# Four half-size pairs at the end of a routed expert layer, and a new place for the weight load

## The chip, the cores and the metric

The kernel runs on one core of one Trainium2 chip. The metric is the device time of one execution in microseconds (us), the median over several runs.

## The reference, cut to what matters

The input is 64 graphs of 256 nodes with 256 features. Two layers follow each other; each is a graph attention step and a feed-forward step, both with a layer norm ahead and a residual added behind. The feed-forward step of the second layer is a mixture of 8 experts, and each token goes to its two best ones:

```python
logits = tokens @ router_w.T
probs = softmax(logits)
rw, re = top_k(probs, 2);  rw = rw / rw.sum(-1, keepdims=True)
combine = zeros((N, E)).at[arange(N)[:, None], re].set(rw)
out = tokens
for e in range(E):                                  # E = 8, D = 256
    h = gelu(tokens @ w1[e] + b1[e], approximate=False)
    y = h @ w2[e] + b2[e]
    out = out + combine[:, e:e + 1] * y
```

The reference computes all experts for all tokens. The kernel computes only the two that count, except for the last three graphs.

## The kernel before, in words

**Graphs.** `batch_layers` takes one graph (256 rows, `NT` = 2 tiles of 128) through the first layer, the second attention and the router's logits. The base of the result (`base`, the token itself) is stored to `out` from there. The first 61 graphs (`ROUTED`) are routed. The last three (`DENSE`) are computed by `dense_expert` with every expert, weighted and summed in SBUF into `dbase`, and stored by `store_dense` at L1075 when the eighth expert is done.

**Routing.** The 61 routed graphs come in chunks of 4, 2 or 1. For each chunk `route` finds the two experts of each token and its place in the expert's region of the DRAM buffer `xs`; `send` (L1094, on POOL) writes the rows there, one indirect DMA of 128 rows at a time. A row of `xs` holds 256 features, the token's number, an expert and two weights.

**Pairs.** Work on experts is cut into pairs: two tiles of 128 rows of one expert (`PAIR` = 256 rows). After a chunk, `allot` computes on DVE which pairs are full, and gives their experts and places as `ids` and `ef`; SP loads them into registers at L919 and L923. As 61 graphs have 61·256 tokens with two rows each, there are 122 pairs' worth of rows. `jobs` hands out full pairs as soon as they are certain to exist, which comes to 122 − 7 = 115. What remains lies in partly filled pairs; after the last chunk, eight writes of `fill` (L1198) put rows of weight zero behind each expert's last row, and `FLUSH` = 2·(8 − 1) = 14 more pairs are taken. Those that no expert needs read a spare region of zero-weight rows. So 129 pairs run in all, the last 14 of them the flush.

**One pair** (`expert_pair`) is, in this order: on SP four DMAs for the rows (`xr`, L930), one for the numbers and weights (`xt`, L941) and one for the expert's first weights (`we`, L959); on DVE the transposition into `sT` (L117); on PE `hidden` (four products of 128 x 256, L992); on ACT a Gelu into `hT` (L998); on PE `product` (L1007) with the resident second weights; on DVE the addition of the bias into `y` (L1017, in `result`); on ACT the scaling by the router's weight (L985); last, `scatter` on POOL.

**Adding to the result.** `scatter` (L1028) issues two indirect DMAs per pair. Each adds 128 rows of 1 KB to `out`, at the rows that `xt` names. As a token's row may occur in two pairs, both DMAs wait for the two of the pair before (`before = added[-2:] + based`): the adding of one pair starts when that of the last has landed. Nine buffers hold `y` (`YBUFS`), seven `we` (`WBUFS`), five `xr` (`XBUFS`), fourteen `xt`.

**Order.** Everything is issued in an order written by the loop at the end of the kernel (`manual_schedule`): in each step every active job goes on to its next `yield`, in the order of the ranks that they give. Each engine works through its own part of that order. Near the end (`SINGLE_AT`) one pair is begun per step while fewer than three wait for their scatter, and one dense job (an expert for one or two of the last graphs) runs beside it.

Of the kernel before, what the change touches and what calls it, by code (L numbers as in the profile page):

```python
# [9 lines left out]
F32 = mybir.dt.float32  # L10
# [5 lines left out]
P = 128  # L16
# [11 lines left out]
def kernel(  # L28
# [749 lines left out]
            dense_batch[b] = dict(base=base, xT=xT)  # L778

    XNG = 8  # L780
    dense_batch, dense_weights = {}, {}

    def dense_home(b):
# [77 lines left out]
    shift = keep.tile([P, E + 1], F32, tag="shift", name="shift")  # L861
    nc.vector.memset(shift, float(E * CAP))

    def allot(c, n, last):

        rt = lambda shape, name, bufs=2, dt=F32: chunk_tile(shape, name, c, bufs, dt)
        vec, tt = nc.vector, nc.vector.tensor_tensor
        full = rt([E], "full")  # L870
        vec.tensor_scalar(
            full, rows[0], 1.0 / PAIR, ((PAIR - 1.0 if last else 0.0) - (PAIR - 1.0) / 2) / PAIR,
            op0=ALU.mult, op1=ALU.add,
        )
        whole(full, full)
        wait = rt([E], "wait")
        tt(wait, full, used, ALU.subtract)
        yield
        ends = rt([E], "ends")
        vec.tensor_tensor_scan(ends, ones[:, :E], wait, 0.0, ALU.mult, ALU.add)  # L880
        start = rt([E], "start")
        tt(start, ends, wait, ALU.subtract)
        tt(shift[:, :E], used, start, ALU.subtract)
        took = rt([E], "took")
        vec.tensor_scalar(took, start, -1.0, float(n), op0=ALU.mult, op1=ALU.add)
        vec.scalar_tensor_tensor(took, took, 0.0, wait, op0=ALU.max, op1=ALU.min)
        tt(used, used, took, ALU.add)
        step = rt([E], "step")
        tt(step, shift[:, 1:], shift[:, :E], ALU.subtract)
        yield  # L890
        past = rt([n, E], "past")
        tt(
            past, ends[:, None, :].to_broadcast([P, n, E]),
            jrow[:, :n, None].to_broadcast([P, n, E]), ALU.is_le,
        )
        ef = rt([n], "ef", 8)
        vec.tensor_reduce(ef, past, AX.X, ALU.add)
        ids = rt([2, n], "ids", 8, I32)
        vec.tensor_scalar(ids[:, 0], ef, float(E - 1), None, op0=ALU.min)
        vec.tensor_scalar(ef, ef, float(E - 1), float(-E), op0=ALU.min, op1=ALU.add)  # L900
        yield
        tt(past, past, step[:, None, :].to_broadcast([P, n, E]), ALU.mult)
        pair_of = rt([n], "pair_of")
        vec.tensor_reduce(pair_of, past, AX.X, ALU.add)
        vec.scalar_tensor_tensor(
            pair_of, pair_of, shift[:, 0:1], jrow[:, :n], op0=ALU.add, op1=ALU.add
        )
        vec.tensor_scalar(ids[:, 1], pair_of, float(E * CAP), None, op0=ALU.min)
        yield ids, ef

    WHY = "counts of at most E (E - 1 at most), and a pair of the regions or the spare one"
    GROUP = 8

    def expert_pair(j, n, ids, ef, regs, needs):

        i = j % GROUP
        upto = min(j + GROUP, n)
        if i == 0:
            _, regs["e"] = nc.values_load_multi_w_load_instructions(  # L919
                ids[0:1, 0, j:upto], engines=[mybir.EngineType.SP], min_val=0, max_val=E - 1,  # L920
                skip_runtime_bounds_check_because=WHY,
            )
            _, regs["t"] = nc.values_load_multi_w_load_instructions(  # L923
                ids[0:1, 1, j:upto], engines=[mybir.EngineType.SP], min_val=0, max_val=E * CAP,
                skip_runtime_bounds_check_because=WHY,
            )
        e_sp, t_sp = regs["e"][i], regs["t"][i]
        xr = io.tile([P, PAIR // S, KT * S], F32, tag="xr", name="xr", bufs=XBUFS)
        loads = [
            nc.sync.dma_start(  # L930
                out=xr[g * S : (g + 1) * S],
                in_=xs_d.rearrange("(t c q) f -> t q c f", c=PAIR // S, q=S)[
                    bass.ds(t_sp, 1), :, :, g * KT * S : (g + 1) * KT * S
                ].rearrange("t q c f -> (t q) c f"),
            )
            for g in range(P // S)
        ]

        xt = small.tile([P, 2, ROW - D], F32, tag="xt", name="xt", bufs=14)
        loads.append(  # L940
            nc.sync.dma_start(  # L941
                out=xt,
                in_=xs_d.rearrange("(t k p) c -> t p k c", p=P, k=2)[
                    bass.ds(t_sp, 1), :, :, D:
                ].rearrange("t p k c -> (t p) k c"),
            )
        )
        for load in loads:
            tc.declare_no_dep(
                load.ins, query=SYNC, group="sent", keep=needs,  # L950
                reason="the pair's rows were sent by these or by sends that earlier loads waited for",
            )
            tc.add_to_no_dep_group("rows", load.ins)
            for ins in needs:
                tc.add_manual_dep(
                    load.ins, ins.name, AFTER, reason="any row of these may lie in the pair"
                )
        we = io.tile([P, WROW], F32, tag="we", name="we", bufs=WBUFS)
        nc.sync.dma_start(  # L959
            out=we, in_=wpack[bass.ds(e_sp, 1), :, :].rearrange("e p c -> (e p) c")  # L960
        )
        yield 90

        yield 95 if more else 75
        xT = turned(work.tile([P, KT, PAIR], F32, tag="sT", name="sT", bufs=3), xr)
        w = small.tile([P, 2], F32, tag="w", name="w", bufs=12)
        yield 30
        yield 30
        hT = hidden(xT, we)
        yield -65  # L970
        nc.vector.scalar_tensor_tensor(
            w[:, :, None], xt[:, :, 1:2], ef[:, j : j + 1], xt[:, :, 2:3],
            op0=ALU.is_equal, op1=ALU.mult,
        )
        nc.vector.tensor_tensor(w[:, :, None], w[:, :, None], xt[:, :, 3:4], ALU.add)
        yield 80
        if i == 0:
            _, regs["x"] = nc.values_load_multi_w_load_instructions(
                ids[0:1, 0, j:upto], engines=[mybir.EngineType.PE, mybir.EngineType.DVE],
                min_val=0, max_val=E - 1, skip_runtime_bounds_check_because=WHY,  # L980
            )
        y = result(hT, bass.ds(regs["x"][i], 1))
        yield 2
        for t in range(2):
            nc.scalar.activation(y[:, t, :], y[:, t, :], AF.Copy, scale=w[:, t : t + 1])  # L985
        scatters.append((y, xt))

    def hidden(xT, we):
        ph = bank("ph", [KT, PAIR])
        for f in range(KT):  # L990
            for k in range(KT):
                nc.tensor.matmul(  # L992
                    ph[:, f, :], we[:, k * D + f * P : k * D + (f + 1) * P], xT[:, k, :],
                    start=(k == 0), stop=(k == KT - 1),
                )
        hT = work.tile([P, KT, PAIR], F32, tag="hT", name="hT", bufs=5)
        for f in range(KT):
            nc.scalar.activation(  # L998
                hT[:, f, :], ph[:, f, :], AF.Gelu, bias=we[:, C_B1 + f : C_B1 + f + 1]
            )  # L1000
        return hT

    def product(hT, e):
        py = bank("py", [2, D])
        for t in range(2):
            for f in range(KT):
                nc.tensor.matmul(  # L1007
                    py[:, t, :], hT[:, f, t * P : (t + 1) * P],
# [4 lines left out]

    def result(hT, e):
        py = product(hT, e)
        y = io.tile([P, 2, D], F32, tag="y", name="y", bufs=YBUFS)
        nc.vector.tensor_add(y, py, b2s[:, e, :].to_broadcast([P, 2, D]))  # L1017
        return y

    scatters, added = [], []  # L1020

    def scatter():

        y, xt = scatters.pop(0)
        before = added[-2:] + based
        based.clear()
        for t in range(2):
            d = nc.gpsimd.indirect_dma_start(  # L1028
                out=out_rows, out_offset=bass.IndirectOffsetOnAxis(
                    ap=xt[:, t, 0:1].bitcast(I32), axis=0  # L1030
# [9 lines left out]
                tc.add_manual_dep(d.ins, ins.name, AFTER, reason="added to before")  # L1040
            tc.add_to_no_dep_group("out", d.ins)
            added.append(d.ins)

    GROUPS = [range(ROUTED, ROUTED + 1), range(ROUTED + 1, B)]

# [66 lines left out]
    def route(c, row0, nt, n, last, xng, lg):  # L1112
# [53 lines left out]
        second_weight(tail[:, :, 2], tail[:, :, 1])  # L1166
        for i, xe in enumerate(xng):
            vec.tensor_copy(xe[:, :, D + 1 :], tail[:, i * NT : (i + 1) * NT, :])
        parts = allot(c, n, False)
        turns = (1, 2, 4, 5) if spread else (0, 1, 2, 3) if nt == 2 * NT else (0, 0, 1, 1)  # L1170
        if last:
            ends_at = rt([E], "ends_at", 2, I32)
# [13 lines left out]
                lambda j=j: expert_pair(j, n, ids, ef, regs, needs) for j in range(n)  # L1186
            )
        if last:
            parts = allot(c + 1, FLUSH, True)
            _, ends_sp = nc.values_load_multi_w_load_instructions(  # L1190
                ends_at[0:1, :], engines=[mybir.EngineType.SP], min_val=0,
                max_val=(E * CAP - 1) * PAIR, skip_runtime_bounds_check_because="rows of a region",
# [2 lines left out]
            for e in range(E):  # L1195
# [12 lines left out]
                nc.sync.nop()  # L1208
                if e % 4 == 3:
                    yield 95  # L1210
            regs2 = {}
            waiting.extend(
                lambda j=j: expert_pair(j, FLUSH, ids2, ef2, regs2, filled)
                for j in range(FLUSH)
            )

# [19 lines left out]
                )  # L1236

    FLUSH = 2 * (E - 1)

    def jobs():  # L1240
        b = done = taken = 0
# [104 lines left out]
```

## Time and the profile before

| | |
|---|---|
| time, median of 6 runs | 1483.56 us (1476.41 to 1485.18) |
| the profiled execution, its own time | 1481.71 us |
| its span, first to last instruction | 1479.9 us (1.8 us lie around it) |
| granted TensorE clock, mean | 0.988 |
| PE busy | 1409.8 us, 95% |
| weight loads (PEld) busy | 1255.5 us, 85% |
| DVE busy | 1238.9 us, 84% |
| ACT busy | 1004.6 us, 68% |
| POOL busy | 862.1 us, 58% |
| scatters (L1028) | 258 DMAs, 414.1 us busy on POOL |

Lines such as L1028 are lines of the kernel's file. "Idle before" in a timeline is the time in which the engine stood still ahead of that instruction, with the event that the profile thinks released it. SPq and POOLq are the sequencers of those engines, which issue DMAs and wait on semaphores without counting as busy.

### The profile page before, as it was taken

The numbers are of one execution on the slowest core, as the hardware profiler recorded it, in microseconds if no ns is written. First come the engines' busy times: TensorE is split into PE (matmuls) and PEld (weight loads), VectorE is DVE, ScalarE is ACT, GpSimd is POOL, SyncE is SP. The second block draws the span as 40 slices with busy tenths as digits, with TensorE's granted clock in tenths as the row PEclk, the third lists the DMA queues.
The fourth block names the chain that finished last, engine by engine and source line by source line (L and its number), as shares of the span: only waits on it lengthen the run. The fifth ranks groups of instructions, "written<-read, shape, count | busy, mean of one in ns | idle before, by whom it ended". The sixth has DMA issues, their size and how long they took to land. (4 is left out here: it accounts for less than half of the span.)

```text
span 1479.9 us, 29895 instructions
## 1 busy us (share of the span) xinstructions
PE 1409.8 (95%) x8046; PEld 1255.5 (85%) x8046; DVE 1238.9 (84%) x4366; ACT 1004.6 (68%) x2389; POOL 862.1 (58%) x851
## 2 busy tenths in 40 slices
PE   7899999999999999999999999999999989989994
PEld 5688888889999999999999999888888878778883
DVE  7789999999999989898999999998888888765542
ACT  1477667677877787777777877677778868643331
POOL 2122446465858676766767685775666768543444
PEclk9999999999999999999999999999999999999998
DMA  4822334576778777777878776777878786798533
GB/s 129 235 86 87 104 121 118 151 186 154 189 178 202 177 186 174 186 171 179 194 185 192 175 186 145 198 186 169 203 149 191 143 181 136 152 226 167 101 44 50
DMA packets 360106, 236.20 MB, mean 160 GB/s; under 512 B 247420, under 2 KB 323204, under 8 KB 359940
## 3 DMA queue, kind: packets, MB, share of 16 engines
q1 hardware_dynamic: 307024, 158.00, 41.7%
q0 software_dynamic: 48864, 66.33, 24.0%
q10 hardware_dynamic: 4052, 9.98, 2.3%
q8 instruction: 66, 1.08, 0.3%
q14 instruction: 100, 0.82, 0.2%
HBM read 146.25 MB, written 87.94 MB: 158 GB/s over the span
## 5 line engine op out<-in xcount | busy, mean ns | idle before, releaser
L1028 POOL DMA_INDIRECT out_dram<-y,xt x258 | 414.1, 1605 | 227.8 <-issue 67.0
L595 PE MATMUL pv<-q,z 128*128 128x65 f32 (+1 forms) x2560 | 360.7, 296 | 0.4
L595 PEld LDWEIGHTS pv<-q,z 128*128 128x128 f32 x2560 | 331.4, 192 | 14.2 <-DVE z L581 0.9
L1094 POOL DMA_INDIRECT xs<-xng,pos x244 | 254.2, 1042 | 65.3 <-issue 58.3
L1007 PE MATMUL py<-w2s,hT 128*128 (+1 forms) x1224 | 283.9, 383 | 6.1 <-ACT hT L998 4.3
L1007 PEld LDWEIGHTS py<-w2s,hT 128*128 128x128 f32 x1224 | 230.4, 191 | 38.6 <-ACT hT L998 7.0
L992 PE MATMUL ph<-sT,we 128*128 128x256 f32 x1032 | 243.2, 385 | 3.3 <-DVE sT L117 1.7
L581 DVE SCALAR_TENSOR_TENSOR z<-z,q,mask 128x256 f32<-128x256 f32 x504 | 231.6, 482 | 16.0 <-DMA z<-terms 7.0
L992 PEld LDWEIGHTS ph<-sT,we 128*128 128x128 f32 x1032 | 197.0, 193 | 31.8 <-DVE sT L117 2.2
L985 ACT ACTIVATE y<-y,w 128x256 f32<-128x256 f32 x258 | 113.1, 498 | 121.1 <-DVE y L1017 120.9
L459 ACT COPY xT<-pt 128x512 f32<-128x512 f32 x209 | 121.0, 587 | 70.4 <-PE pt L453 67.9
L504 PE MATMUL pq<-wx,xT 128*128 128x259 f32 x512 | 127.1, 391 | 15.2 <-ACT xT L459 15.2
L406 POOL TENSOR_SCALAR rstd<-mv 128x4 f32<-128x4 f32 (+1 forms) x66 | 15.6, 236 | 215.8 <-DVE mv L379 165.0
L424 ACT ACTIVATE off<-x,sums 128x256 f32<-128x256 f32 x256 | 129.3, 505 | 13.2 <-DVE x L678 7.5
L1017 DVE TENSOR_TENSOR y<-py,b2s 128x512 f32<-128x512 f32 x129 | 86.0, 686 | 53.8 <-PE py L1007 42.7
L469 PE MATMUL pq<-wx,xT 128*128 128x268 f32 x512 | 128.8, 395 | 1.8 <-ACT xT L459 0.7
L504 PEld LDWEIGHTS pq<-wx,xT 128*128 128x128 f32 x512 | 96.1, 192 | 34.7 <-ACT xT L459 21.0
L998 ACT ACTIVATE hT<-ph,we 128x256 f32<-128x256 f32 x258 | 103.9, 471 | 30.8 <-PE ph L992 26.3
L671 PE MATMUL pf<-wfT,xT 128*128 128x256 f32 x512 | 122.3, 382 | 0.0
L469 PEld LDWEIGHTS pq<-wx,xT 128*128 128x128 f32 x512 | 98.4, 193 | 21.3 <-DVE wx L168 1.4
L712 ACT ACTIVATE rel<-pv,rinv 128x256 f32<-128x256 f32 x128 | 53.9, 468 | 88.2 <-DVE rinv L602 87.8
L671 PEld LDWEIGHTS pf<-wfT,xT 128*128 128x128 f32 x512 | 93.7, 193 | 10.1
(173 smaller groups left out, 2366.0 us busy)
## 6 DMA issues: line engine op xcount, KB each, us to landing
we<-wpack SPq DMA_DIRECT2D x129, 264.0 KB
xr<-xs SPq DMA_DIRECT2D x516, 64.0 KB
z<-terms SPq DMA_DIRECT2D x46, 512.0 KB
xin<-in_x_dram SPq DMA_DIRECT2D x64, 256.0 KB
out_dram<-base SPq DMA_DIRECT2D x61, 256.0 KB
xblk<-in_x_dram SPq DMA_DIRECT2D x188, 64.0 KB
z<-terms ACTq DMA_DIRECT2D x17, 512.0 KB
z<-terms SPq DMA_DIRECT2D x46, 128.0 KB
```

The lines of the kernel that those rows point to most:

```text
L424: nc.scalar.activation(off, src[:, t, :], AF.Square, bias=sums[:, t : t + 1], scale=-float(D), accum_out=sq[:, at + t : at + t + 1],)
L459: nc.scalar.copy(dst, pt)
L469: nc.tensor.matmul(pq.rearrange("p h c -> p (h c)"), xT[:, k, t * P : (t + 1) * P], wx[:, k, :], start=(k == 0), stop=(k == KT - 1),)
L504: nc.tensor.matmul(pq, xT[:, k, t * P : (t + 1) * P], wx1[:, k, :], start=(k == 0), stop=(k == KT - 1),)
L581: nc.vector.scalar_tensor_tensor(z[:, j, :, h, :], terms, q[:, j, h, HD + 2 : HD + 3], masks[0][:, j, :].rearrange("p (t i) -> p t i", t=N ...
L595: nc.tensor.matmul(pv[:, h, :], z(j, h, t), q[:, j, h, : d + 1], start=(j == 0), stop=(j == NT - 1),)
L671: nc.tensor.matmul(pf[:, t, :], xT[:, k, t * P : (t + 1) * P], wfT[:, k, :], start=(k == 0), stop=(k == KT - 1),)
L985: nc.scalar.activation(y[:, t, :], y[:, t, :], AF.Copy, scale=w[:, t : t + 1])
L992: nc.tensor.matmul(ph[:, f, :], we[:, k * D + f * P : k * D + (f + 1) * P], xT[:, k, :], start=(k == 0), stop=(k == KT - 1),)
L1007: nc.tensor.matmul(py[:, t, :], hT[:, f, t * P : (t + 1) * P], w2s[:, e, f * D : (f + 1) * D].rearrange("p e c -> p (e c)"), start=(f == 0 ...
L1028: d = nc.gpsimd.indirect_dma_start(out=out_rows, out_offset=bass.IndirectOffsetOnAxis(ap=xt[:, t, 0:1].bitcast(I32), axis=0), in_=y[:, t, ...
L1094: d = nc.gpsimd.indirect_dma_start(out=xs_d[: E * CAP * PAIR, :], out_offset=bass.IndirectOffsetOnAxis(ap=at, axis=0), in_=xe, in_offset=None,
```

## The change

It has four parts.

- The last four of the 14 flush pairs hold one tile of 128 rows in place of two. Their loads, products, Gelus, scalings and scatters cover 128 rows; each issues one scatter DMA.
- So that what is left fits, `allot_rest` takes the place of `allot` for the flush: it lists first the pairs that hold more than 128 rows (at most `WHOLE` = 10) and then those with 1 to 128.
- In `expert_pair`, for all 129 pairs, `we` is loaded ahead of `xr` and `xt`, and an `nc.sync.nop()` follows the loads.
- For the flush pairs, the load of `we` gets a dependence on the last scatter of an earlier pair, taken from a new list `ended` with one entry per scattered pair. By its name `BEHIND` it is the eleventh pair ahead.

```diff
+    BEHIND, flush_regs = 11, {}
...
+    def allot_rest(c, n):
+        rt = lambda shape, name, dt=F32: chunk_tile(shape, name + "_r", c, 1, dt)
+        vec, tt = nc.vector, nc.vector.tensor_tensor
+        base = rt([3, E], "base")
+        vec.tensor_copy(base[:, 0], used)
+        for i, more_rows in ((1, P - 1.0), (2, PAIR - 1.0)):
+            vec.tensor_scalar(
+                base[:, i], rows[0], 1.0 / PAIR, (more_rows - (PAIR - 1.0) / 2) / PAIR,
+                op0=ALU.mult, op1=ALU.add,
+            )
+        whole(base[:, 1:], base[:, 1:])
+        wait = rt([2, E], "wait")
+        tt(wait, base[:, 1:], base[:, :2], ALU.subtract)
...                                  # as in allot, over 2 * E entries in place of E
-    def expert_pair(j, n, ids, ef, regs, needs):
+    def expert_pair(j, n, ids, ef, regs, needs, tiles=2):
...
+        we = io.tile([P, WROW], F32, tag="we", name="we", bufs=WBUFS)
+        d = nc.sync.dma_start(
+            out=we, in_=wpack[bass.ds(e_sp, 1), :, :].rearrange("e p c -> (e p) c")
+        )
+        at = ROUTED * NT * P // PAIR - (E - 1) + j - BEHIND
+        if regs is flush_regs and at < len(ended):
+            tc.add_manual_dep(
+                d.ins, ended[at].name, AFTER, reason="keeps loads out of the adding of earlier pairs"
+            )
         xr = io.tile([P, PAIR // S, KT * S], F32, tag="xr", name="xr", bufs=XBUFS)
...
-        we = io.tile([P, WROW], F32, tag="we", name="we", bufs=WBUFS)
-        nc.sync.dma_start(
-            out=we, in_=wpack[bass.ds(e_sp, 1), :, :].rearrange("e p c -> (e p) c")
-        )
+        nc.sync.nop()
...
-        for t in range(2):
+        for t in range(tiles):
             nc.scalar.activation(y[:, t, :], y[:, t, :], AF.Copy, scale=w[:, t : t + 1])
...
     def scatter():
-        for t in range(2):
+        for t in range(y.shape[1]):
             d = nc.gpsimd.indirect_dma_start(
...
+        ended.append(d.ins)
...
-            parts = allot(c + 1, FLUSH, True)
+            parts = allot_rest(c + 1, FLUSH)
...
-                lambda j=j: expert_pair(j, FLUSH, ids2, ef2, regs2, filled)
+                lambda j=j: expert_pair(
+                    j, FLUSH, ids2, ef2, regs2, filled, 2 if j < WHOLE else 1
+                )
...
+    WHOLE = (PAIR * (E - 1) + E * (PAIR - P - 1)) // PAIR
```

More of the change, by code (lines that the diff above doesn't have):

```diff
@@ L862, with allot @@
     nc.vector.memset(shift, float(E * CAP))
-    def allot(c, n, last):
+    def allot(c, n):
         rt = lambda shape, name, bufs=2, dt=F32: chunk_tile(shape, name, c, bufs, dt)
@@ L871, in allot @@
         vec.tensor_scalar(
-            full, rows[0], 1.0 / PAIR, ((PAIR - 1.0 if last else 0.0) - (PAIR - 1.0) / 2) / PAIR,
-            op0=ALU.mult, op1=ALU.add,
+            full, rows[0], 1.0 / PAIR, -(PAIR - 1.0) / 2 / PAIR, op0=ALU.mult, op1=ALU.add
         )
@@ L909, in allot @@
         yield ids, ef
+    def allot_rest(c, n):
[11 more added lines that the diff above has]
+        tt(wait, base[:, 1:], base[:, :2], ALU.subtract)
+        yield
+        flat = lambda t: t.rearrange("p a e -> p (a e)")
+        ends = rt([2 * E], "ends")
+        vec.tensor_tensor_scan(ends, ones[:, : 2 * E], flat(wait), 0.0, ALU.mult, ALU.add)
+        start = rt([2 * E], "start")
+        tt(start, ends, flat(wait), ALU.subtract)
+        shift = rt([2 * E + 1], "shift")
+        vec.memset(shift[:, 2 * E :], float(E * CAP))
+        tt(shift[:, : 2 * E], flat(base[:, :2]), start, ALU.subtract)
+        step = rt([2 * E], "step")
+        tt(step, shift[:, 1:], shift[:, : 2 * E], ALU.subtract)
+        yield
+        past = rt([n, 2 * E], "past")
+        tt(
+            past, ends[:, None, :].to_broadcast([P, n, 2 * E]),
+            jrow[:, :n, None].to_broadcast([P, n, 2 * E]), ALU.is_le,
+        )
+        of = rt([n], "of")
+        vec.tensor_reduce(of, past, AX.X, ALU.add)
+        ef = rt([n], "ef")
+        vec.tensor_scalar(ef, of, float(E), float(-E), op0=ALU.is_ge, op1=ALU.mult)
+        tt(ef, ef, of, ALU.add)
+        ids = rt([2, n], "ids", I32)
+        vec.tensor_scalar(ids[:, 0], ef, float(E - 1), None, op0=ALU.min)
+        vec.tensor_scalar(ef, ef, float(E - 1), float(-E), op0=ALU.min, op1=ALU.add)
+        yield
+        tt(past, past, step[:, None, :].to_broadcast([P, n, 2 * E]), ALU.mult)
+        pair_of = rt([n], "pair_of")
+        vec.tensor_reduce(pair_of, past, AX.X, ALU.add)
+        vec.scalar_tensor_tensor(
+            pair_of, pair_of, shift[:, 0:1], jrow[:, :n], op0=ALU.add, op1=ALU.add
+        )
+        vec.tensor_scalar(ids[:, 1], pair_of, float(E * CAP), None, op0=ALU.min)
+        yield ids, ef
@@ L927, in expert_pair @@
         e_sp, t_sp = regs["e"][i], regs["t"][i]
+        we = io.tile([P, WROW], F32, tag="we", name="we", bufs=WBUFS)
[6 more added lines that the diff above has]
+                d.ins, ended[at].name, AFTER, reason="keeps loads out of the adding of earlier pairs"
+            )
         xr = io.tile([P, PAIR // S, KT * S], F32, tag="xr", name="xr", bufs=XBUFS)
@@ L930, in expert_pair @@
             nc.sync.dma_start(
-                out=xr[g * S : (g + 1) * S],
+                out=xr[g * S : (g + 1) * S, : tiles * P // S],
                 in_=xs_d.rearrange("(t c q) f -> t q c f", c=PAIR // S, q=S)[
-                    bass.ds(t_sp, 1), :, :, g * KT * S : (g + 1) * KT * S
+                    bass.ds(t_sp, 1), :, : tiles * P // S, g * KT * S : (g + 1) * KT * S
                 ].rearrange("t q c f -> (t q) c f"),
@@ L941, in expert_pair @@
             nc.sync.dma_start(
-                out=xt,
+                out=xt[:, :tiles],
                 in_=xs_d.rearrange("(t k p) c -> t p k c", p=P, k=2)[
-                    bass.ds(t_sp, 1), :, :, D:
+                    bass.ds(t_sp, 1), :, :tiles, D:
                 ].rearrange("t p k c -> (t p) k c"),
@@ L957, in expert_pair @@
                 )
-        we = io.tile([P, WROW], F32, tag="we", name="we", bufs=WBUFS)
-        nc.sync.dma_start(
-            out=we, in_=wpack[bass.ds(e_sp, 1), :, :].rearrange("e p c -> (e p) c")
-        )
+        nc.sync.nop()
         yield 90
         yield 95 if more else 75
-        xT = turned(work.tile([P, KT, PAIR], F32, tag="sT", name="sT", bufs=3), xr)
+        xT = work.tile([P, KT, PAIR], F32, tag="sT", name="sT", bufs=3)
+        xT = turned(xT[:, :, : tiles * P], xr[:, : tiles * P // S])
         w = small.tile([P, 2], F32, tag="w", name="w", bufs=12)
@@ L971, in expert_pair @@
         nc.vector.scalar_tensor_tensor(
-            w[:, :, None], xt[:, :, 1:2], ef[:, j : j + 1], xt[:, :, 2:3],
+            w[:, :tiles, None], xt[:, :tiles, 1:2], ef[:, j : j + 1], xt[:, :tiles, 2:3],
             op0=ALU.is_equal, op1=ALU.mult,
         )
-        nc.vector.tensor_tensor(w[:, :, None], w[:, :, None], xt[:, :, 3:4], ALU.add)
+        nc.vector.tensor_tensor(
+            w[:, :tiles, None], w[:, :tiles, None], xt[:, :tiles, 3:4], ALU.add
+        )
         yield 80
@@ L981, in expert_pair @@
             )
-        y = result(hT, bass.ds(regs["x"][i], 1))
+        y = result(hT, bass.ds(regs["x"][i], 1))[:, :tiles]
         yield 2
-        for t in range(2):
+        for t in range(tiles):
             nc.scalar.activation(y[:, t, :], y[:, t, :], AF.Copy, scale=w[:, t : t + 1])
@@ L988, in hidden @@
     def hidden(xT, we):
-        ph = bank("ph", [KT, PAIR])
+        n = xT.shape[-1]
+        ph = bank("ph", [KT, n])
         for f in range(KT):
@@ L995, in hidden @@
                 )
-        hT = work.tile([P, KT, PAIR], F32, tag="hT", name="hT", bufs=5)
+        hT = work.tile([P, KT, PAIR], F32, tag="hT", name="hT", bufs=5)[:, :, :n]
         for f in range(KT):
@@ L1003, in product @@
     def product(hT, e):
-        py = bank("py", [2, D])
-        for t in range(2):
+        tiles = hT.shape[-1] // P
+        py = bank("py", [tiles, D])
+        for t in range(tiles):
             for f in range(KT):
@@ L1015, in result @@
         py = product(hT, e)
-        y = io.tile([P, 2, D], F32, tag="y", name="y", bufs=YBUFS)
-        nc.vector.tensor_add(y, py, b2s[:, e, :].to_broadcast([P, 2, D]))
+        tiles = py.shape[1]
+        y = io.tile([P, 2, D], F32, tag="y", name="y", bufs=YBUFS)[:, :tiles]
+        nc.vector.tensor_add(y, py, b2s[:, e, :].to_broadcast([P, tiles, D]))
         return y
-    scatters, added = [], []
+    scatters, added, ended = [], [], []
     def scatter():
@@ L1026, in scatter @@
         based.clear()
-        for t in range(2):
+        for t in range(y.shape[1]):
             d = nc.gpsimd.indirect_dma_start(
@@ L1168, in route @@
             vec.tensor_copy(xe[:, :, D + 1 :], tail[:, i * NT : (i + 1) * NT, :])
-        parts = allot(c, n, False)
+        parts = allot(c, n)
         turns = (1, 2, 4, 5) if spread else (0, 1, 2, 3) if nt == 2 * NT else (0, 0, 1, 1)
@@ L1210, in route @@
                     yield 95
-            regs2 = {}
+            regs2 = flush_regs
             waiting.extend(
-                lambda j=j: expert_pair(j, FLUSH, ids2, ef2, regs2, filled)
+                lambda j=j: expert_pair(
+                    j, FLUSH, ids2, ef2, regs2, filled, 2 if j < WHOLE else 1
+                )
                 for j in range(FLUSH)
```

## The prediction

> **What bounds the kernel now.** I read the page first. PE is busy for 95% of the span, but the slices show that this ends early: the last tenth has little DVE, ACT and DMA work. So I went to the end of the chain of waits, then to POOL's timeline, because the last piece of the chain is POOL's. The chain, restricted to the last microseconds:
>
> ```profile
> 1460.53 2.55 DMA out_dram<-dbase
> 1463.08 0.01 issue
> 1463.09 1.55 POOL out_dram L1028
> ...
> 1470.28 1.55 POOL out_dram L1028
> 1471.83 1.86 POOLq L1341
> ```
>
> The chain steps from the store of a dense graph to POOL's scatter at 1463.09. I don't believe that step: a scatter doesn't depend on that store (L1075 is declared free of it), only on the scatters of the pair before. POOL's timeline (start, duration, what, idle time before it) shows the real rhythm:
>
> ```profile
> 1369.70 1.55 POOL L1028 DMA_INDIRECT out_dram<-y,xt  x1 [3.11 <-ACT hT L998]
> 1371.56 1.56 POOL L1028 DMA_INDIRECT out_dram<-y,xt  x1 [0.30 <-ACT hT L998]
> 1377.73 1.55 POOL L1028 DMA_INDIRECT out_dram<-y,xt  x1 [4.62 <-DMA out_dram<-y,xt]
> ...
> 1450.08 1.55 POOL L1028 DMA_INDIRECT out_dram<-y,xt  x1 [3.05 <-DMA out_dram<-y,xt]
> 1451.94 1.56 POOL L1028 DMA_INDIRECT out_dram<-y,xt  x1 [0.30 <-issue]
> 1456.61 1.55 POOL L1028 DMA_INDIRECT out_dram<-y,xt  x1 [3.12 <-ACT hT L998]
> 1458.47 1.56 POOL L1028 DMA_INDIRECT out_dram<-y,xt  x1 [0.30 <-issue]
> 1463.09 1.55 POOL L1028 DMA_INDIRECT out_dram<-y,xt  x1 [3.06 <-DMA out_dram<-dbase]
> 1464.95 1.56 POOL L1028 DMA_INDIRECT out_dram<-y,xt  x1 [0.30 <-issue]
> 1470.28 1.55 POOL L1028 DMA_INDIRECT out_dram<-y,xt  x1 [3.77 <-issue]
> 1472.14 1.56 POOL L1028 DMA_INDIRECT out_dram<-y,xt  x1 [0.30 <-issue]
> ```
>
> Two scatter DMAs per pair, 0.30 apart, then about 3.05 of standing still, whoever is named as the releaser. That is the landing of the pair before. One pair costs 1.55 + 0.30 + 1.56 + 3.05 = 6.46 us. Are the scatters waiting for data? DVE's timeline has the last two `y`:
>
> ```profile
> 1434.47 0.69 DVE L1017 TENSOR_TENSOR y<-py,b2s 128x512 f32<-128x512 f32 x1 [2.99 <-PE py L1007]
> 1439.65 0.69 DVE L1017 TENSOR_TENSOR y<-py,b2s 128x512 f32<-128x512 f32 x1 [1.59 <-PE py L1007]
> ```
>
> The last `y` is there at 1440.3, its scatter starts at 1470.28: 30 us, over four pairs, of backlog. So the chain of scatters alone sets the end. The other end, the dense graphs, is earlier. PE's and SP's timelines:
>
> ```profile
> 1460.89 1.99 PE L1007 MATMUL py<-w2s,hT 128*128 128x256 f32 x8 [0.62 <-ACT hT L998]
> ```
> ```profile
> 1386.69 0.36 SPq L959 DMA_DIRECT2D we<-wpack  x1
> 1460.53 4.74 SPq L1075 DMA_DIRECT2D out_dram<-dbase  x2
> ```
>
> The last store is issued by 1465.3; the chain gives such a store 2.55 us to land, so this end is at 1467.8, while POOL issues until 1473.7. The two SP lines also say that no load is issued after 1387.
>
> **The change part by part.** *Four scatters fewer.* Call the pairs 0 to 128; 125 to 128 become half pairs, with scatters at 1450.08, 1456.61, 1463.09 and 1470.28. Each loses its second DMA: 0.30 + 1.56 = 1.86 us, on the path. The wait of 3.05 behind it has to follow a single DMA now, which this trace never shows. From below: the shortest such idle time on POOL in the last 100 us is 2.87 (at 1404.88), so a half pair would take 4.42, 2.04 less than 6.46. From above: if the first DMA of a pair is the one that lands last, the cadence stays 6.46 for three intervals and only the last pair's 1.86 is saved. I take 3.05, because the rows show it behind an identical DMA of 128 rows over and over: 4.61 per half pair, 4 × 1.86 = 7.44 saved. The last interval before is 7.19, with an idle time of 3.77; I leave its extra 0.7 in, and it may vanish (a gain of 0.7).
>
> The Trainium skill, page "DMA: Bandwidth & Descriptors", section on the anatomy of a DMA on the gpsimd path, speaks against this: a DMA there costs about 2.0 us whatever its size, plus its bytes over 436 GB/s, so halving a transfer saves next to nothing. By that rule alone, 128 KB fewer would save an estimated 0.3 us per pair, 1.2 in all: 1482.4, no measurable change. The rows above decide otherwise for this kernel, since here a whole DMA goes, and POOL's issue of it is serial.
>
> From POOL's last issue (1473.70) to the end of the span lie 6.2 us; the chain shows POOL's queue at L1341 there. I keep them.
>
> *Lighter loads.* Pairs 125 to 128 are loaded between 1369 and 1387. Scatters started from 1354 to 1385 come at intervals of 8.60, 6.53, 8.03 and 7.64; from 1392 on, with no loads, at 6.3 to 6.5. Half of `xr` is gone from four loads while `we` stays. The two intervals that lie in these loads (8.03, 7.64) exceed 6.46 by 2.8 together; between none and half of it can be won. I take 0.5.
>
> *PE, DVE and ACT.* PE loses two of four products at L1007 and half the columns at L992 in each of four pairs. A full pair's two steps take 1.73 each by the distance of the rows, so 4 × 1.73 = 6.9 us at most. This lies wholly beside the scatters: it moves the dense end from 1467.8 towards 1461, while the new last scatter issue ends at 1473.7 − 7.4 = 1466.3. Even if PE saved nothing, 1467.8 is no later than POOL's last landing (the rows give 3.05 behind 1466.3), so the cover holds. I count zero.
>
> *`allot_rest`.* It has 21 DVE instructions for 19. Such rows take 0.17 us, the wide ones 0.27; with 224 entries in place of 112 I add 0.1 to each of four. About 0.8 us, on DVE near 1300. The first flush pair's rows were loaded at 1320.5 and first used at 1330.9, and the scatter backlog at that time was 30 us. Zero; without that cover it would cost 0.8.
>
> *`we` ahead of `xr`, and a nop.* For 129 pairs `xr` is issued some 0.55 us later (0.36 for the issue, 0.2 to the next), and its packets queue behind 264 KB of `we`: at the 189 GB/s that the windows view gives for 1296 to 1385 that is 1.4 us. Together 2 us at worst. Its user is the transposition on DVE. In the trace the time from the last `xr` issue to `sT` is 16 us in the median and at least 6.6, with one exception of 3.0 (pair 113). The waits of tile `sT` list one wait on rows, in the whole run (us, times):
>
> ```profile
>   DMA xr<-xs: 0.8, 1
> ```
>
> One pair of 129 has no slack. Its loss of 2 us sits on DVE, and its `ph` came 10.7 us after `sT`, so PE doesn't feel it. The nop costs SP at most some 0.05 by the size of its small instructions (semaphore events here are 0.02 to 0.03), and SP is not on the path. I take zero for both, bounds −1 and +3 us.
>
> *The new wait.* Here I compute the index. `ROUTED * NT * P // PAIR` is 61·2·128 // 256 = 61, not 122, since each token has two rows and this counts one. So `at` = 61 − 7 + j − 11 = 43 + j, while flush pair j is pair 115 + j. The load waits for the 72nd pair ahead, which landed hundreds of us earlier: nothing. If it were the eleventh, everything behind `we` on SP would wait too (rows, the next pairs' loads, the dense store). The last load would go at about 1404 (landing of pair 117) for a use at 1417.7, so PE would still not wait, but three scatters after 1387 would meet loads: 3 × (7.6 − 6.46) = 3.4 lost, and the same order won before 1385. I take zero, ±3.4.
>
> **Sum.** 7.44 + 0.5 = 7.9 us. The profiled execution, 1481.71, becomes 1473.8 (span 1472.0). It lies 1.85 below the median of the runs; from the median the same step gives 1483.56 − 7.9 = 1475.7.
>
> **The rivals.**
> - *The landing sets the cadence* (same): a half pair takes nearly 6.46, as both DMAs land together. Against it: all idle times behind second DMAs are alike, 2.9 to 3.1, as if counted from the second. Saves 1.9: 1481.7.
> - *Rows come late in the body* (slower): with `we` in front, `xr` misses its transposition, and DVE, which works in order, carries it on to PE at 95%. Price 2 us per pair hit; it outweighs the gain from four pairs, and shows as slower from seven (14 − 7.9 = 6). With a tenth of the pairs, 13: 1483.6 − 7.9 + 26 = 1502. Against it: slack of at least 6.6 in 128 of 129.
> - *The wait does bite at eleven pairs*, the change doing what its name says: 1475.7 ± 3.4, at worst 1479.1.
>
> **How the numbers follow.** A change within 0.3% (4.5 us) can't be told from none here; faster means below 1479.1. Forecast 0.72, cadence 0.10, late rows 0.09, biting wait 0.09 (two thirds of it still faster). Faster 0.72 + 0.06 = 0.78; same 0.10 + 0.03 = 0.13; slower 0.09. The forecast with its bounds spans 1473.3 (7.44 + 1.4 + 0.7 + 4 × 0.18 won) to 1479; runs of one kernel differ by several us, so I reach to 1471.5, and above to 1482, which takes in the cadence case.
>
> **What would show it.** POOL's timeline should have four single scatters at the end, 4.6 apart, and the span should end 6.2 behind the last issue. SP's load of `we` should carry no visible wait, and its last load should again be issued near 1387. PE should be done by about 1456. Starts 6.4 apart for single scatters would make the cadence rival right; idle time of DVE before `sT` put down to `xr`, the late rows; loads after 1395, the biting wait.

## The result, and the profile after

The changed kernel takes 1476.3 us, median of 19 runs (1467.99 to 1479.83); the kernel before, now with 40 runs, 1483.51 (1476.41 to 1487.98). The medians differ by 7.2 us. The ratio estimated from all runs is 0.9946 with a 95% interval of 0.9934 to 0.9957, which is 6.4 to 9.8 us. Forecast were 1475.7 us and a gain of 7.9.

The profiled execution took 1478.87 us with a span of 1476.9, so the two profiles differ by 3.0 us in their spans and the medians by 7.2. This execution was slower than the median, and it was late long before the end: pair 115's scatter starts at 1389.36 where it started at 1385.37 before, pair 125's at 1455.33 instead of 1450.08. The end has therefore to be read from a landmark inside each trace. POOL's timeline of the changed kernel (start, duration, what, idle time before it):

```profile
1448.93 1.55 POOL L1089 DMA_INDIRECT out_dram<-y,xt  x1 [3.04 <-DMA out_dram<-y,xt]
1450.79 1.56 POOL L1089 DMA_INDIRECT out_dram<-y,xt  x1 [0.30 <-issue]
1455.33 1.55 POOL L1089 DMA_INDIRECT out_dram<-y,xt  x1 [2.98 <-ACT hT L1057]
1459.86 1.56 POOL L1089 DMA_INDIRECT out_dram<-y,xt  x1 [2.97 <-ACT hT L1057]
1464.42 1.55 POOL L1089 DMA_INDIRECT out_dram<-y,xt  x1 [3.00 <-issue]
1468.93 1.56 POOL L1089 DMA_INDIRECT out_dram<-y,xt  x1 [2.96 <-issue]
```

The last whole pair has its two DMAs 0.30 apart; then come four single ones, 4.5 us from start to start, with the same idle time of 3.0 before each. From the first of these four to the end of the span are 1476.9 − 1455.33 = 21.6 us; before, 1479.9 − 1450.08 = 29.8. The tail is 8.2 us shorter.

Nothing else has moved onto the path. DVE's timeline has the last `y`, PE's the last product, SP's the last load and the dense stores:

```profile
1438.35 0.42 DVE L1078 TENSOR_TENSOR y<-py,b2s 128x256 f32<-128x256 f32 x1 [0.72 <-ACT hT L1057]
```
```profile
1459.60 1.99 PE L1067 MATMUL py<-w2s,hT 128*128 128x256 f32 x8 [0.62 <-ACT hT L1057]
```
```profile
1388.88 0.35 SPq L978 DMA_DIRECT2D we<-wpack  x1
...
1459.23 4.75 SPq L1137 DMA_DIRECT2D out_dram<-dbase  x2
```

The last `y` still waits 30 us for its scatter (1438.8 to 1468.93). PE ends at 1461.6, nine us ahead of the end of POOL's last issue (1470.5). SP's loads are issued by 1392; before it was 1387, in a trace that was some 5 us earlier there.

### The profile page after: what moved, and what is told of

It is laid out like the page before. It is cut to its first block, busy times and chain, and to the rows that moved or that the text cites. A ratio compares the mean times of both kernels' runs of the same rounds, so it can differ in the third digit from the quotient of the medians.

```text
span 1476.9 us, 29795 instructions
## 1 busy us (share of the span) xinstructions
PE 1404.5 (95%) x8030; PEld 1251.1 (85%) x8030; DVE 1238.4 (84%) x4368; ACT 1002.6 (68%) x2385; POOL 856.0 (58%) x847
## 3 DMA queue, kind: packets, MB, share of 16 engines
q0 software_dynamic: 48288, 65.81, 23.6%
## 5 line engine op out<-in xcount | busy, mean ns | idle before, releaser
L1089 POOL DMA_INDIRECT out_dram<-y,xt x254 | 408.2, 1607 | 237.4 <-issue 61.7
L1067 PE MATMUL py<-w2s,hT 128*128 (+1 forms) x1208 | 280.7, 383 | 4.6 <-ACT hT L1057 4.6
L1067 PEld LDWEIGHTS py<-w2s,hT 128*128 128x128 f32 x1208 | 227.3, 192 | 37.8 <-ACT hT L1057 8.1
L1051 PE MATMUL ph<-sT,we 128*128 128x256 f32 (+1 forms) x1032 | 238.6, 380 | 4.9 <-DVE sT L117 2.0
L1051 PEld LDWEIGHTS ph<-sT,we 128*128 128x128 f32 x1032 | 193.8, 192 | 32.5 <-DVE sT L117 2.5
L1078 DVE TENSOR_TENSOR y<-py,b2s 128x512 f32<-128x512 f32 (+1 forms) x129 | 84.9, 677 | 48.3 <-PE py L1067 35.6
L1057 ACT ACTIVATE hT<-ph,we 128x256 f32<-128x256 f32 (+1 forms) x258 | 103.2, 469 | 28.5 <-PE ph L1051 24.0
L469 PEld LDWEIGHTS pq<-wx,xT 128*128 128x128 f32 x512 | 96.9, 190 | 21.6 <-DVE xT L117 1.8
```

The source lines that it names most:

```text
L469: nc.tensor.matmul(pq.rearrange("p h c -> p (h c)"), xT[:, k, t * P : (t + 1) * P], wx[:, k, :], start=(k == 0), stop=(k == KT - 1),)
L1051: nc.tensor.matmul(ph[:, f, :], we[:, k * D + f * P : k * D + (f + 1) * P], xT[:, k, :], start=(k == 0), stop=(k == KT - 1),)
L1067: nc.tensor.matmul(py[:, t, :], hT[:, f, t * P : (t + 1) * P], w2s[:, e, f * D : (f + 1) * D].rearrange("p e c -> p (e c)"), start=(f == 0 ...
L1089: d = nc.gpsimd.indirect_dma_start(out=out_rows, out_offset=bass.IndirectOffsetOnAxis(ap=xt[:, t, 0:1].bitcast(I32), axis=0), in_=y[:, t, ...
```

## The experiments

Four chips were used. The kernel before took 1504.4, 1500.6, 1481.1 and 1500.7 us on them, so times are compared as ratios to it, and profiles by the distance from pair 125's scatter to the end of the span, called the tail. These are the kernels that leave the place of the scatters in POOL's order as it was:

| kernel | scatters of the last four | ratio, 95% interval | pair 125's scatter to the end, us |
|---|---|---|---|
| before | two each | 1 | 29.8 |
| order_only | two each | 0.9987 (0.9965 to 1.0008) | 30.6 |
| two_scatters | two each | 0.9995 (0.9977 to 1.0013) | 30.9 |
| changed | one each | 0.9946 (0.9934 to 0.9957) | 21.6 |
| changed_again | one each | 0.9935 (0.9915 to 0.9954) | 21.5 |
| half_only | one each | 0.9927 (0.9903 to 0.9951) | 21.5 |
| one_scatter | one each | 0.9943 (0.9924 to 0.9962) | 21.7 |
| eleven | one each | 0.9938 (0.9914 to 0.9962) | 22.0 |
| changed_third | one each | 0.9939 (0.9915 to 0.9963) | 21.2 |

The theory was that the four missing scatter DMAs are the whole gain. Its rivals: the lighter compute and loads carry it; the new order of loads costs something; the wait matters.

**half_only**: the half pairs and `allot_rest`, without the other two parts.

```diff
-        we = io.tile(...)                       # ahead of xr, with its dependence
-        d = nc.sync.dma_start(out=we, ...)
...
-        nc.sync.nop()
+        we = io.tile(...)                       # behind xr and xt, as before
+        nc.sync.dma_start(out=we, ...)
```

> The half pairs and the new allotment alone; the weight load stays behind the rows, with no nop and no dependence. My theory (four scatter DMAs of 1.86 us go from the chain that sets the end, the rest of the change is neutral): 1476, 7.5 us under the kernel before, four single scatters 4.6 us apart at the end. Rival 'late rows' (the new place of the weight load costs the body a few us, which the changed kernel pays and this one does not): 1471 to 1473.

Measured: 1493.47 beside 1504.43, ratio 0.9927. The tail is that of the changed kernel. As ratios, the theory's 1476 is 0.995 and the rival's 1471 to 1473 are 0.992 to 0.993: the measured ratio lies with the rival, and its interval takes in both. So this run doesn't tell the two apart; the next one measures the order of loads by itself.

**order_only**: the kernel before, with `we` ahead of `xr` and the nop.

> The kernel before with the weight load ahead of the rows and the nop behind them, for all 129 pairs; whole pairs to the end. My theory: no change, 1483.5 within 2 us. Rival 'late rows': 1486 or more, with pair 125's scatter starting some us later than 1450 in the profile and more idle time of DVE before the transposition.

Measured: 1501.53 beside 1504.43, ratio 0.9987 with an interval up to 1.0008. No loss: the rival's 1486 would have been a ratio of 1.0017 or more. The waits of tile `sT` in this run (us, times):

```profile
  DMA xr<-xs: 5.0, 2
```

Two transpositions of 129 waited for rows, 5.0 us in total, where one waited 0.8 before. Such waits occur with either order: half_only, with the rows in front, has one of 2.4 us, and the three profiles of the changed kernel have two of 0.9 in all, one of 2.4 and one of 2.0. That the new order makes rows late isn't shown, then; in these profiles one or two pairs are hit at most, where the prediction put the point of decision at seven.

**one_scatter**: whole loads and whole compute to the end, but one scatter for each of the last four pairs, whose second tile holds only filling rows.

```diff
-    def expert_pair(j, n, ids, ef, regs, needs, tiles=2):
+    def expert_pair(j, n, ids, ef, regs, needs, parts=2):
+        tiles = 2
...
-        scatters.append((y, xt))
+        scatters.append((y[:, :parts], xt))
```

> The changed kernel, but its last four pairs load and compute 256 rows as before and only their scatter covers 128 (the second tile of these pairs holds nothing but filling rows of weight zero, so nothing is lost). My theory (only the scatters count, the lighter loads give 0.5, PE nothing): 1476 to 1477, scatters 4.6 us apart. Rival 'PE and loads carry the gain': close to the kernel before, 1481 to 1483.

Measured: 1495.20, ratio 0.9943, tail 21.7. POOL's timeline of this run:

```profile
1470.30 1.56 POOL L1091 DMA_INDIRECT out_dram<-y,xt  x1 [2.98 <-DMA out_dram<-y,xt]
1474.79 1.56 POOL L1091 DMA_INDIRECT out_dram<-y,xt  x1 [2.94 <-issue]
1479.36 1.55 POOL L1091 DMA_INDIRECT out_dram<-y,xt  x1 [3.01 <-issue]
1483.99 1.56 POOL L1091 DMA_INDIRECT out_dram<-y,xt  x1 [3.08 <-issue]
```

The whole gain is there without any saving on PE, ACT, DVE or in the loads, as far as the interval and the tail can tell.

**two_scatters**: the counterpart, with everything halved except the number of scatter DMAs. Each half pair issues a second one of 128 rows that adds zeros to a DRAM buffer which nobody reads.

```diff
-        for t in range(y.shape[1]):
+        for t in range(2):
             d = nc.gpsimd.indirect_dma_start(
-                out=out_rows, ...
+                out=out_rows if t < y.shape[1] else nowhere, ...
-                in_=y[:, t, :], ...
+                in_=y[:, t, :] if t < y.shape[1] else nothing, ...
```

> The changed kernel with half loads and half the compute in the last four pairs, but each of them still issues a second scatter DMA of 128 rows, which adds zeros to a DRAM buffer that nobody reads. My theory: the gain is gone, 1483 (0.5 us of lighter loads at most), scatter pairs 6.45 us apart to the end. Rival 'PE and loads carry the gain': 1476 to 1478. Rival 'the landing of fewer rows in the result is what got shorter': intervals near 5.5.

Measured: 1502.96, ratio 0.9995. POOL's timeline:

```profile
1472.48 1.70 POOL L1094 DMA_INDIRECT out_dram<-y,xt  x1 [3.09 <-DMA out_dram<-y,xt]
1474.48 1.56 POOL L1094 DMA_INDIRECT nowhere<-fill  x1 [0.30 <-issue]
1479.16 1.56 POOL L1094 DMA_INDIRECT out_dram<-y,xt  x1 [3.12 <-DMA nowhere<-fill]
1481.02 1.79 POOL L1094 DMA_INDIRECT nowhere<-fill  x1 [0.30 <-issue]
1486.10 1.56 POOL L1094 DMA_INDIRECT out_dram<-y,xt  x1 [3.29 <-DMA nowhere<-fill]
1487.96 1.56 POOL L1094 DMA_INDIRECT nowhere<-fill  x1 [0.30 <-issue]
1493.27 1.56 POOL L1094 DMA_INDIRECT out_dram<-y,xt  x1 [3.75 <-issue]
```

With the second DMA back, the gain is gone, although PE was done at 1479.4, 24 us before the end of this span. The pairs come 6.7, 6.9 and 7.2 us apart, a little wider than the 6.45 expected. The runs of this kernel show a granted clock of 0.976 to 0.982, under the 0.979 to 0.987 of the kernel before on this chip, so its time alone is weak evidence; the tail is not, as PE does nothing in its last 24 us.

With one_scatter this shows that the second scatter DMA of these pairs carries the gain, and the work in the pairs none of it that can be seen. One thing stays together in all of these runs: a DMA that goes takes its 128 KB with it. No run changes the bytes at the same number of DMAs, so the two can't be told apart here.

**eleven**: the dependence on the pair that really is eleven ahead.

```diff
-        at = ROUTED * NT * P // PAIR - (E - 1) + j - BEHIND
+        at = 2 * ROUTED * NT * P // PAIR - (E - 1) + j - BEHIND
```

> The changed kernel with the index of the dependence doubled in its first term (122 in place of 61), so that the load of flush pair 115 + j waits for the landing of pair 104 + j, the eleventh ahead. My theory: the last load goes some 15 to 20 us later, scatters before it come closer together and scatters beside it further apart, PE doesn't wait; within 3.4 us of the changed kernel. Rival 'the wait is worth something': 3 us or more under the changed kernel, as loads and scatters share the DMA engines more evenly. Rival 'the wait bites': DVE idle before the transposition and a time over the changed kernel by 3 us or more.

Measured: 1490.61 beside 1500.56, ratio 0.9938, against 1490.82 and 0.9935 for the changed kernel on the same chip. Now the wait exists; SP's own waits (total us, times, longest) say so, and its timeline shows the last loads 6.4 to 6.5 us apart, the last one 17 us later than in changed_again (1401.32):

```profile
SPq L978 <- DMA out_dram<-y,xt: 25.3, 10, 4.1
```
```profile
1405.55 0.35 SPq L978 DMA_DIRECT2D we<-wpack  x1
1412.07 0.35 SPq L978 DMA_DIRECT2D we<-wpack  x1
1418.44 0.35 SPq L978 DMA_DIRECT2D we<-wpack  x1
```

In the changed kernel's list no wait of L978 for a scatter occurs. Holding the loads back costs nothing and brings nothing that these intervals can show: in the profiles the twenty scatters from pair 105 to 125 come 6.91 us apart with the wait and 7.10 without, 4 us over the stretch, from one execution each.

**changed_again** is the changed kernel beside eleven and early.

> The changed kernel as it is, beside the other two on the same chip: 0.9946 of the kernel before, single scatters 4.5 us apart at the end, 21.6 us from the first of them to the end of the span, where kernels with two scatters per pair take 29.8 to 30.9.

Measured: 0.9935, tail 21.5, as expected.

**early**: the backlog suggests a further step. In the kernel before, the chain of scatters is 17 us behind `y` at pair 105; part of that may be only its place in POOL's order.

```diff
         scatters.append((y, xt))
+        if order_steps[-1] >= SINGLE_AT:
+            yield -97
+            while scatters:
+                scatter()
...
-            if scatters:
+            if scatters and step < SINGLE_AT:
```

> The changed kernel, but in the last nine graphs a pair's scatters are placed on POOL in the same step in which its y is scaled, not in the next. The chain of scatters sets the end and it enters the flush with a lag of some 18 us behind y (pair 105: y at 1290.8, scatter at 1308.3 in the kernel before). My theory: if part of that lag is only the place in POOL's order, the chain starts up to 7 us earlier and the end comes up to 6 us earlier (then the dense graphs set it). Rival 'the lag is landing waits and not order': the time of the changed kernel. Rival: POOL's norm work now waits behind scatters and the body gets longer, 3 us or more over the changed kernel.

Measured: 1498.21 beside 1500.56, ratio 0.9989, so 7 us over the changed kernel. The lag did shrink (pair 115: 13 us in place of the 31 of changed_again), and POOL was done early, but PE was late:

```profile
1484.20 1.55 POOL L1093 DMA_INDIRECT out_dram<-y,xt  x1 [2.96 <-issue]
```
```profile
1495.09 1.99 PE L1071 MATMUL py<-w2s,hT 128*128 128x256 f32 x8 [0.62 <-ACT hT L1061]
```

The span ends at 1502.5, 5.4 us behind PE's last product. The windows view says when PE lost it: from 1000 to 1100 us PE was busy for 85.5 us here and 94.0 in changed_again, from 1100 to 1200 for 97.3 and 98.9. That is around the step from which the scatters stand earlier in POOL's order. The timelines of POOL, ACT and PE in that stretch show the wait:

```profile
1014.70 1.62 POOL L1093 DMA_INDIRECT out_dram<-y,xt  x1 [4.16 <-DMA out_dram<-base]
1016.62 1.77 POOL L1093 DMA_INDIRECT out_dram<-y,xt  x1 [0.31 <-issue]
1022.71 1.55 POOL L1093 DMA_INDIRECT out_dram<-y,xt  x1 [4.31 <-DMA out_dram<-y,xt]
1024.56 1.54 POOL L1093 DMA_INDIRECT out_dram<-y,xt  x1 [0.30 <-issue]
1029.18 1.55 POOL L1093 DMA_INDIRECT out_dram<-y,xt  x1 [3.08 <-DMA out_dram<-y,xt]
1031.04 1.57 POOL L1093 DMA_INDIRECT out_dram<-y,xt  x1 [0.30 <-issue]
1032.68 0.20 POOL L444 TENSOR_SCALAR rstd<-sq 128x4 f32<-128x4 f32 x1
1032.96 1.04 POOL L447 TENSOR_TENSOR rstd<-rstd,mhalf 128x4 f32<-128x4 f32 x1
```
```profile
1034.03 0.26 ACT L511 ACTIVATE ex<-pq,rstd 128x3 f32<-128x3 f32 x1 [16.01 <-POOL rstd L447]
```
```profile
1034.71 7.09 PE L595 MATMUL pv<-q,z 128*128 128x65 f32 x32 [10.24 <-ACT ex L511]
```

Three pairs are scattered one after another, with their waits for landing; the norm's `rstd` comes behind them on POOL, ACT stands still for it for 16.0 us and PE behind ACT for 10.2. In changed_again no wait of PE in these 100 us is longer than 2.5. So the third rival, norm work behind scatters, is what this trace shows, at a price of 7 us in the medians; the profiled execution is the slowest of its twelve.

**early_last2** and **early_dense** do the same from the last two graphs on (step `TICKS * (B - 2)`), and from the end of the last graph's start on (`TICKS * B`).

> The changed kernel with scatters placed in the same step as their y, but only from the last two graphs on instead of the last nine, so that the body keeps POOL's order. My theory: the chain of scatters enters the flush up to one step (7 us) earlier, and the end comes 2 to 6 us before the changed kernel's, until the dense graphs set it (their last store is issued some 6 us ahead of POOL's last issue). Rival 'the lag is landing waits': the time of the changed kernel, 0.9935 to 0.9946 of the kernel before.

> The same from the end of the last graph's start on. My theory: by then the chain is already saturated and only the queue gets longer, so no gain over the changed kernel; 0.9935 to 0.9946 of the kernel before. Rival 'order still counts here': 3 us or more under it.

Measured beside 1481.1: 1472.87 (0.9943, 0.9925 to 0.9962) and 1476.08 (0.9962, 0.9947 to 0.9978). early_dense lies a little above its forecast of 0.9935 to 0.9946. In early_last2 the end of the profile is indeed shorter: the last scatter is issued ahead of PE's last product, and from the last dense product at L1055 to the end are 8.5 us where the changed kernel has 18. Its ratio is no lower, though, so it was run once more beside the changed kernel on one chip, with a third kernel that adds the wait of eleven.

**changed_third, early_last2_b, early_eleven**

> The changed kernel once more, beside the next two on one chip: 0.9935 to 0.9946 of the kernel before; in the profile POOL's last issue comes well behind the end of the dense graphs, some 18 us from PE's last products at L1051 to the end of the span.

> Scatters in the same step as their y from the last two graphs on, as before, now beside the changed kernel. Its first profile had the scatters done ahead of the dense graphs (8.5 us from PE's last products at L1055 to the end, where the changed kernel had 18.2), yet its ratio was no lower than those of the changed kernel on other chips. My theory: the tail is really 6 to 9 us shorter, but PE's path lost a part in the steps where POOL's norm work waits behind scatters; 3 to 6 us under the changed kernel. Rival 'all given back': no difference.

> Both: scatters in the same step from the last two graphs on, and the dependence on the pair that is really eleven ahead. My theory: the same time as early_last2_b, since PE's path sets the end in both and no load waits long enough to reach it. Rival 'spread loads help the body's last graphs': 2 us or more under it.

Measured beside 1500.7: 1491.77 (0.9939, 0.9915 to 0.9963), 1493.19 (0.9947, 0.9925 to 0.9969) and 1490.08 (0.9933, 0.9910 to 0.9956). No difference that these intervals show, where 3 to 6 us were expected; the rival 'all given back' fits. Where it was given back stays open. The 8.5 us came again, and in the profile the body from pair 60 on is only 2.6 us longer than in changed_third. But the profiled execution of early_last2_b took 1484.68 us, the shortest of its eight, with a granted clock of 0.990 where most of the others had 0.981 to 0.985, so it may not be typical. None of these versions beats the changed kernel clear of noise.

## Why the prediction was right, point by point

- **What bounds the kernel.** The chain of scatters, as read from POOL's timeline and the backlog of `y`, against the step in the chain of waits that named the dense store. two_scatters shows it: all compute of the last four pairs lighter, a tail of 30.9 us and no gain.
- **Four scatters fewer.** The term was 4 × 1.86 = 7.44. Measured from the first of the four to the end of the last issue: 1473.70 − 1450.08 = 23.6 before, 1470.49 − 1455.33 = 15.2 after: 8.5. The term was too small by 1.0, and two rows say why. The idle time before a single DMA is 2.96 to 3.00 where it was 3.05 to 3.12; and the last interval's extra 0.7, which I had left in as something that may vanish, did vanish. It returned where there were two DMAs per pair (idle 3.75 before the last pair of two_scatters; 4.09 in order_only).
- **"That is the landing of the pair before"** was only part of it. The chain of two_scatters splits such an idle time, here before pairs 125 and 128:

```profile
1467.83 3.81 DMA out_dram<-y,xt
...
1471.77 0.71 issue
1472.48 1.70 POOL out_dram L1094
...
1487.96 3.77 DMA nowhere<-fill
...
1491.86 1.42 issue
1493.27 1.56 POOL out_dram L1094
```

The piece called DMA begins with its issue, so by this chain it has landed 2.2 us behind the end of that issue (3.81 − 1.56). Then some 0.8 pass, mostly "issue", in which the profile names nothing that POOL waits for. The extra 0.7 ahead of the last pair lies in this second part, 1.42 in place of 0.71, and not in the landing. The kernel before shows the same ahead of its last pair:

```profile
1464.95 3.79 DMA out_dram<-y,xt
...
1468.86 1.42 issue
1470.28 1.55 POOL out_dram L1028
```

Why the second part is longer there stays open.

- **The cadence rival** (both DMAs land together, so one costs as much as two) is out: 4.5 us from start to start, not 6.4.
- **The rule of the Trainium skill, page "DMA: Bandwidth & Descriptors"**, section on the anatomy of a DMA on the gpsimd path, a fixed cost of about 2 us and little for the bytes: taken as a saving of bytes it gave 1482.4, and measured were 1476.3. The page gives it per DMA, and what went here was a whole DMA with its own 1.86 us of serial issue, so the result doesn't contradict it. The idle time ahead of the next scatter stayed at 3.0 behind one DMA as behind two, but each DMA still carries 128 KB; how its cost goes with its bytes no run here shows.
- **The end behind the last issue.** 6.2 kept; 6.4 measured.
- **Lighter loads, 0.5.** Not shown. one_scatter has the whole loads and the same ratio; a half microsecond is below what these intervals resolve. The scatters from pair 105 to 125 come 7.09 us apart before and 7.07 to 7.18 in the changed kernel's three profiles, so none of it shows there.
- **The sum.** 7.9 were forecast; the tail of the profiles is 8.2 shorter and the medians are 7.2 apart. That it comes so close is in part luck: one term was 1.0 too small, another of 0.5 isn't shown, and the end behind the last issue took 0.2 back.
- **PE, counted at zero.** PE did save what was worked out, in one execution each: from pair 115's transposition to the last dense product 129.0 us before, 122.0 after, 7.0 for the 6.9. The products over 128 columns follow each other at 0.112 us, those over 256 at 0.216. None of it reached the end.
- **`we` ahead of `xr`, and the nop, counted at zero.** order_only's interval, 0.9965 to 1.0008, includes zero and leaves out the +3 us of the bounds.
- **`allot_rest`, zero.** Never isolated; half_only contains it and keeps the gain.
- **The wait.** The index points 72 pairs back, and the trace has no wait for a scatter at that load. eleven shows that at the intended distance it would be harmless too: 1490.61 beside 1490.82 us, inside the ±3.4 given.
- One expectation for the profile was off: PE was to be done by 1456 and was at 1461.6. The estimate left out that the body of another execution can be 5 us later; counted from pair 115 it fits.

## What to carry to other kernels

When a serial chain of DMAs with a wait for landing between them sets the end, count the DMAs in the chain and take one out; halving the arithmetic behind them had no effect here. Find that chain by the distance between a result's production and its send (30 us here) and by the equal idle times before each issue, not by whom a waits view names as the releaser. Compare two profiles by distances from a landmark within each, since their spans can differ by 5 us ahead of the part that was changed. And an index in a dependence is worth working out by hand: this one had no effect because it counted one row per token where there are two.

## What the runs showed of the hardware

An indirect DMA that adds 128 rows of 1 KB holds POOL for 1.55 to 1.56 us in most rows above (up to 1.8 in some), and the next one starts 0.30 us later. Where each waits for the landing of the last, with no loads beside them, one costs 4.5 us from start to start and two cost 6.4 to 6.5.

In early_last2_b the runs with a granted TensorE clock of 0.990 took 1484.68 and 1487.61 us, those with 0.981 to 0.982 took 1495.74 to 1497.19, which is as far apart as the effect of the change or farther. The tie is looser elsewhere: runs of the changed kernel with 0.987 took 1467.99 to 1479.83 us, those with 0.982 took 1476.16 to 1478.87. Nor is it shown that the clock is the cause. It is a mean over the span, and it is low where PE stands still: 0.71 from 1020 to 1040 us in early, where PE is busy for 9.8 of 20 us (1.00 in changed_again, with 18.4), and 0.59 from 1480 to 1503 in two_scatters, where PE does nothing. The four chips of the experiments differed by up to 1.6% for the same kernel (1481.1 to 1504.4).
